# A four-layer graph network with a planned instruction order: q's factor moved into the copies, layer 2's statistics on ScalarE, six of eight divisions on ScalarE, other ranks

## Chip, cores and metric

The kernel runs on one core of a Trainium2 chip. The metric is the device time of one execution in microseconds; the time before is 3005.9 us, the median of three runs (3004.96 to 3010.77). The engines are named as in the profile: PE is TensorE (matmuls), PEld its weight loads, DVE is VectorE, ACT is ScalarE, POOL is GpSimd, and SP issues most DMAs.

## What is computed

The input x has 128 batches of 128 nodes with 512 features, all in 32-bit floats. Four layers follow, each with a residual sum and a layer norm; `adj` is one 128 x 128 matrix that all batches share.

```python
x = layernorm(x + (adj @ x) @ weight + bias)                 # layer 0
h = x @ W; e = leaky_relu(s1[:, None] + s2[None, :]) * adj   # layer 1: s1, s2 = h @ a1, h @ a2
x = layernorm(x + elu(softmax(e) @ h + beta * h))
x = layernorm(x + max over the last axis of relu(pre))       # layer 2, from adj and b
q, k, v = x @ w_qkv                                          # layer 3: 8 heads of 64
o = softmax(where(adj == 0, -inf, q @ k.T * 64**-0.5)) @ v
o = o @ w_proj + b_proj
x = layernorm(x + o + (o - mean(o)) * rstd(o) * gamma + beta)
```

In layer 2 the same matrix serves as W1 and W2, so its result for a node is one number: the greatest of its mixed features plus b, and at least 0. It is added to all 512 features of the node.

## The kernel before

A batch is a tile of 128 nodes by 512 features in one large SBUF tile, the arena, which is cut into units of 256 columns. Each of the 128 batches is a Python generator, `batch(i)`, that yields a request for an engine (`use("ACT", 0.48)`), with its cost in microseconds and the buffers it needs, and then issues instructions. The class `Plan` runs all generators at build time: it keeps a time for each engine and buffer, takes the request that can start first (ties go by urgency, then by rank, where a lower rank is served first), and so writes out the order in which each engine's instructions stand. The costs are multiplied by `SLACK` (1.1 for ACT, 1.05 for DVE), PE requests are planned `MARGIN` after their inputs are ready, and a request's rank is mostly the number of its batch, shifted by `SOFT`, `PROJ`, `SECTION` and, for the last groups, `SOON`. On the chip each engine works through its list in this fixed order and waits where an input is late.

The products with 512 x 512 weights are done for two batches at a time with seven block products instead of eight (`seven`, a Strassen-Winograd scheme). It needs sums of weight blocks, made once on POOL (`sums`, line 584), and differences of data blocks, made on POOL for each product (`differences`, line 901). The block products of layers 0, 1 and of the projection are issued at line 914, those of layer 3's q, k and v at line 963 (`section`, for a group of four batches). Their results come out of PSUM by an ACT copy (lines 818 and 881) and by a DVE addition onto what was copied before (805, 811, or 801 where a row sum is taken along). The chain is copy, next PE product, addition, so PE is tied to ACT and DVE within each product.

What a batch does, with its lines:

- Layer 0: mixing by `adj` on PE (386 with a transpose on DVE and a round trip through DRAM, or 367), products (914, or 359 for the first twelve batches), the bias on POOL (352), then `layernorm_sums`: ACT makes the squares with an accumulated sum (340), a small ACT instruction the variance (342), POOL its power of -0.5 (306), ACT the bias of the norm (345) and the norm (346). DVE only scales the row sum (335 or 337).
- Layer 1: logits on DVE (1142, 734 to 761) with exponentials on ACT (749) and two DMA round trips, mixing (367), products (914), ELU (1166, 1168, 1183), `layernorm_sums`.
- Layer 2: mixing (1193), the maximum on DVE (1196, 1199), its addition on ACT (1207), then `layernorm_dve`: DVE takes the statistics (293, 299, 301), POOL the power (306), DVE the norm (323).
- Layer 3: a transpose (1214) and a DMA round trip, q, k and v (963), scores (1040), the mask (1231), the maximum over each head's row (1239), eight exponentials on ACT with accumulated sums (1253), the reciprocal (1259), eight ACT instructions that multiply by it (1267), transposes (1271), a DMA round trip, the product with v (1061), a copy (1302), the projection (914; 359 and 1433 for the last four batches), and the two norms (1406, 1410, `layernorm_sums`, store at 1416).

The switches in question stand at the top of the file. `SCALED` is the number of heads whose division is done on ACT; the others are divided by one DVE instruction. `SUMS2` chooses for layer 2 between `layernorm_sums` (1) and `layernorm_dve` (0). `WHOLE` is the number of last batches whose softmax is done over all heads at once. `GUESTS` is the number of first batches whose input may lie in any free part of the arena. `RUN` holds batch i back until the group `RUN` before its own has its layer 3 inputs. `APART` is the number of last groups whose products with v are requested by themselves (`attend`), not in turns with the next group's scores (`tiled`).

The scale of the scores, 64 ** -0.5, is put into q's weights once, on POOL, before the weight sums of layer 3 are made:

```python
yield use("POOL", 5.8)
nc.gpsimd.tensor_scalar(
    wqkv_sb[:, :, :D], wqkv_sb[:, :, :D], HD**-0.5, None, op0=ALU.mult
)
```

Of the kernel before, what the change touches and what calls it, by code (L numbers as in the profile page):

```python
# [9 lines left out]
AF = mybir.ActivationFunctionType  # L10
ALU = mybir.AluOpType
# [5 lines left out]
D = 512  # L17
K = D // P
G = 4
APART = 6  # L20
FIRST = 0
PAIRS = 2
SOON = (0, 0, -2, 8, 12, 18)
WHOLE = 0
KEPT = 7
ATTENDS = 2
RUN = 8
SEVEN0 = 1
SUMS2 = 0
SCALED = 8  # L30
SEVEN1 = 1
SEVENP = 1
PLAIN = 4
GUESTS = 10
STICK = 0.4
CLOSE = 2900
SOFT = 10
PROJ = -6
SECTION = 12
PACE = 0  # L40
EAGER = 8
H = 8
HD = D // H
# [8 lines left out]
UNIT = 256  # L52
CAPS = {"x": 9, "xr": 2, "yT": 8, "v": 4, "qk": 10, "xT": 4}
SIZES = {"u": 1, "t": 2, "x": 2, "early": 2, "xr": 2, "yT": 2, "v": 4, "qk": 4, "xT": 4}
LAST, AHEAD = 16, 6
DIRECT = 12
LATER = 3
LANDED = 2.2
# [5 lines left out]
SP_ = 1.1  # L64
SLACK = {"PE": 1.0, "DVE": DVE_, "ACT": ACT_, "POOL": POOL_, "SP": SP_}
BORDERS = 0.1
MARGIN = 0.7
LAND, ROW_LAND = 2.8, 0.0053


# [158 lines left out]
def gnn_stack_kernel(  # L229
# [252 lines left out]
    def loads():  # L482
        yield use("SP", 0.4)
        adj_slot.append((yield use("SP", 0.0, "t")))
        adj_sb = buf(adj_slot[0], D)[:, :P]
        adj_slot.append(adj_sb)
        nc.sync.dma_start(adj_sb, adj)
        landing(adj_in, P // 4)
        yield from load(0, "ACT", nc.scalar)
        w0_slot.extend((yield use("SP", 0.0, lambda: ("qk", "qk"))))  # L490
        halves = [buf(slot, 2, D) for slot in w0_slot]
        w0_nat.extend(halves[k // 2][:, k % 2] for k in range(K))
        for k in range(K):
            yield use("SP", 0.43)
            nc.sync.dma_start(w0_nat[k], w0[k * P : (k + 1) * P])
            landing(w0_chunk[k], P)
        yield from load(1)
        yield use("SP", 0.43)
        nc.sync.dma_start(bias0_sb, rows(bias0, D))
        landing(bias0_in, P)  # L500
        for i in range(2, 4):
            yield from load(i)
        slot = yield use("SP", 1.1, "qk")
        matrix(w1_sb, w1)
        a_sb = buf(slot, 2, D)
        nc.sync.dma_start(a_sb, rows(a, 2 * D).rearrange("p (s f) -> p s f", s=2))
        landing(w1_in, (K + 2) * P)
        plan.start(logit_rows(a_sb, slot), 0)
        for i in range(4, 8):
            yield from load(i)  # L510
        yield use("SP", 5.6)
        permuted(w0_sb, w0)
        landing(w0_in, K * P)
        plan.start(layer0_sums(), 0)
        yield use("SP", 1.0)
        nc.sync.dma_start(beta1_sb, rows(beta1, 1))
        nc.sync.dma_start(
            b2_sb, bass.AP(tensor=b2.tensor, offset=b2.offset, ap=[[1, P], [1, 1]])
        )
        landing(scalars_in, 2 * P)  # L520
        for i in range(8, 14):
            yield from load(i)
        yield use("SP", 6.3)
        permuted(wqkv_sb, w_qkv)
        matrix(wproj_sb, w_proj)
        for dst, src in ((bproj_sb, b_proj), (gamma_sb, gamma), (beta3_sb, beta3)):
            nc.sync.dma_start(dst, rows(src, D))
        landing(w3_in, (4 * K + 3) * P)
        plan.start(weight_sums(), 0)
        for i in range(14, NB):  # L530
            yield from load(i)

# [53 lines left out]
    def weight_sums():  # L586

        yield w3_in
        yield use("POOL", 5.8)
        nc.gpsimd.tensor_scalar(  # L590
            wqkv_sb[:, :, :D], wqkv_sb[:, :, :D], HD**-0.5, None, op0=ALU.mult
        )
        for s in range(3):
            yield from sums(s)
        done(w3_ready)
        if SEVENP:
            yield from sums(4)
        done(wproj_ready)
# [192 lines left out]
        gr.xT[2] = buf(gr.slot["xT", 2], 1, 2, n)  # L791
        yield from differences(gr.block, gr.have, gr.used, 0.18 + 0.58 * gr.half, gr.first)

    def seven(rank, bx, wide, time, multiply, parts, finished, have, home, housed, slow=0.0, into=None):

        copy, sum_ = (0.45, 0.6) if wide == D else (0.24, 0.33)
        copy, sum_ = copy + slow, sum_ + slow

        def total(a, c, i, j):
            if into:  # L800
                nc.vector.scalar_tensor_tensor(  # L801
                    c, a, 1.0, c, op0=ALU.mult, op1=ALU.add, accum_out=into[j][i]
                )
            else:
                nc.vector.tensor_tensor(c, a, c, op=ALU.add)  # L805

        def kept(p, i, j, event):
            if into:
                yield use("DVE", sum_, urgent=True)
                for a, c in parts(p, i, j):  # L810
                    nc.vector.tensor_tensor(c, a, c, op=ALU.add)
                done(event)
                return
            got = yield use("ACT", copy, lambda: home(j), urgent=True)
            if got:
                housed(j, got)
            for a, c in parts(p, i, j):
                nc.scalar.copy(c, a)  # L818
            done(event)

        def keep(p, i, j):
            event = Event()
            plan.start(kept(p, i, j, event), rank)
            return event

        def added(p, kept, i, j, event):
            yield kept
            yield use("DVE", sum_, urgent=True)
            for a, c in parts(p, i, j):
                total(a, c, i, j)  # L830
            finished(j)
            done(event)

        def add(p, kept, i, j):
            event = Event()
            plan.start(added(p, kept, i, j, event), rank)
            return event

        def release(event, bank):
            yield event  # L840
            give(bank)

        x = bank(bx, D)[:, :wide]
        multiply(x, A11, B11, True)
        m1 = keep(x, 0, 0)

        bz = yield use("PE", time, "ps")
        z = bank(bz, D)[:, :wide]
        multiply(z, A12, B21, True, True)
        plan.start(release(add(z, m1, 0, 0), bz), rank)  # L850

        yield m1
        yield have[T2]
        yield use("PE", time)
        multiply(x, S2, T2)
        u2 = keep(x, 1, 0)

        yield have[T3]
        by = yield use("PE", time, "ps")
        y = bank(by, D)[:, :wide]  # L860
        multiply(y, S3, T3, True)
        yield u2
        yield have[T1]
        yield use("PE", time)
        multiply(x, S1, T1)
        u4 = keep(x, 1, 1)
        c22 = add(y, u4, 1, 1)
        yield u4
        yield use("PE", time)
        multiply(x, S4, B22, final=True)  # L870

        def last(bx):
            if into:
                yield use("DVE", sum_, urgent=True)
            else:
                yield use("ACT", copy, urgent=True)
            for a, c in parts(x, 0, 1):
                if into:
                    total(a, c, 0, 1)
                else:  # L880
                    nc.scalar.copy(c, a)
            give(bx)
            finished(1)

        plan.start(last(bx), rank)
        yield c22
        yield have[T4]
        yield use("PE", time)
        multiply(y, A22, T4, final=True)
        plan.start(release(add(y, u2, 1, 0), by), rank)  # L890
# [51 lines left out]
    def section(gr, s, before):  # L942
# [51 lines left out]
        def housed(j, got):  # L994
# [8 lines left out]
        done(gr.begun[s])  # L1003
        yield from seven(
            gr.first, bx, wide, time, multiply, parts, finished, gr.have, home, housed,
            0.0 if s == 2 or half == 1 else 0.07,
        )

    def tiled(gr, before, bs):
        yield gr.qk  # L1010
        waiting = list(range(before.size)) if before else []
        for b in waiting:
            yield before.rows[b]

        steps = [(score, bs[:2])]
        steps += [(attends, waiting[b : b + 2]) for b in range(0, len(waiting), 2)]
        steps += [(score, bs[b : b + 2]) for b in range(2, len(bs), 2)]
        was = None
        for do, batches in steps:
            n = len(batches)  # L1020
            slots = yield use(
                "PE", 0.87 * n, lambda: ("ps",) * (n if do is attends else 2 * n),
                late=0.0, urgent=True, follow=was is not None, kind=do.__name__,
            )
            was = do
            if do is attends:
                attends(before, batches, slots)
                continue
            for m, b in enumerate(batches):
                score(gr, b, slots[2 * m : 2 * m + 2])  # L1030
                done(gr.scored[b], 0.2 - 0.87 * (n - 1 - m))
# [58 lines left out]
    def batch(i):  # L1090
# [169 lines left out]
        if SCALED < H:  # L1260
# [2 lines left out]
                rs[:, SCALED:, None].to_broadcast([P, H - SCALED, P]), op=ALU.mult,  # L1263
            )
        for j in range(SCALED):
            yield use("ACT", 0.2)
            nc.scalar.activation(pr[:, j, :], pr[:, j, :], AF.Identity, scale=rs[:, j : j + 1])  # L1267
        halves = yield use("DVE", 1.22, lambda: ("t", "t"))
        turned = [buf(bt, Q, H // 2, S) for bt in halves]
# [250 lines left out]
```

## Time and profile before

| what | us |
|---|---|
| median of three runs | 3005.9 |
| the profiled execution | 3009.2 |
| its span, first to last instruction | 3007.5 |
| ACT, exponentials (line 1253), 1024 instructions | 404.8 |
| ACT, divisions (line 1267), 1024 instructions | 373.7 |
| DVE, statistics (line 293), 255 instructions | 173.8 |
| POOL, powers (line 306), 383 + 257 instructions | 247.1 + 166.3 |
| POOL, q's factor (line 590), one instruction | 5.5 |

The granted TensorE clock is 0.995 of full speed on average. HBM moves 142 GB/s, the DMA engines are busy about half of the time. A busy time is a sum over the records of a group; consecutive ACT instructions overlap by about 0.1 us in the records, so the time from one start to the next is a little shorter than the mean of one.

### The profile page before, as it was taken

What the parts mean: (1) busy time and instruction counts of PE and PEld (TensorE: products, weight loads), DVE (VectorE), ACT (ScalarE), POOL (GpSimd) and SP (SyncE); (2) the same over time, 40 slices, a digit from 0 to 9 for tenths busy, and PEclk for the clock granted to TensorE, in tenths of its full rate; (3) what the DMA queues carried; (4) which work ended last, traced back from release to release, by engine and by line L of the source; (5) the groups of instructions that cost most, each with busy time, mean ns of one, the idle gap of its engine ahead of it and who ended that gap; (6) DMA issues with size and microseconds to landing.
All of it is one profiled execution on the core that took longest, in us unless ns stands there. A gap on an engine that the chain in (4) does not pass through costs nothing. (4 is left out here: it accounts for less than half of the span.)

```text
span 3007.5 us, 54842 instructions
## 1 busy us (share of the span) xinstructions
PE 2950.5 (98%) x16503; PEld 2476.7 (82%) x16503; DVE 2554.8 (85%) x6023; ACT 2209.8 (73%) x6916; POOL 1886.0 (63%) x2050
## 2 busy tenths in 40 slices
PE   9899999999999999999999999999999999999997
PEld 5688788888888888888888888888888888888886
DVE  7998788888988888988898888988988988888676
ACT  4568677777677777777776777676886767777696
POOL 7855566566657666667565666656665655765545
PEclk9999999999999999999999999999999999999999
DMA  5445455355545555654555544646455644654353
GB/s 210 101 117 161 115 163 156 106 146 157 154 137 145 145 144 155 167 137 150 132 153 144 156 137 121 162 135 164 146 139 148 169 128 120 175 142 131 89 148 123
DMA packets 884104, 430.83 MB, mean 143 GB/s; under 512 B 572128, under 2 KB 785760, under 8 KB 883808
## 3 DMA queue, kind: packets, MB, share of 16 engines
q1 hardware_dynamic: 865376, 393.75, 48.6%
q10 hardware_dynamic: 18432, 33.56, 3.0%
q8 instruction: 133, 2.18, 0.3%
q14 instruction: 163, 1.34, 0.1%
HBM read 222.36 MB, written 204.80 MB: 142 GB/s over the span
## 5 line engine op out<-in xcount | busy, mean ns | idle before, releaser
L901 POOL TENSOR_TENSOR arena<-arena 128x256 f32<-128x256 f32 (+1 forms) x868 | 764.8, 890 | 300.3 <-PE ps L914 93.0
L914 PE MATMUL ps<-wsum_sb,arena 128*128 128x256 f32 x2208 | 553.5, 383 | 17.8 <-POOL arena L901 7.8
L914 PEld LDWEIGHTS ps<-wsum_sb,arena 128*128 128x128 f32 x2208 | 414.7, 191 | 105.9 <-issue 17.6
L914 PE MATMUL ps<-w_sb,arena 128*128 128x256 f32 x1952 | 489.7, 379 | 4.7 <-DVE arena L805 2.8
L306 POOL TENSOR_TENSOR sums<-sums,neghalf 128x1 f32<-128x1 f32 x383 | 247.1, 648 | 376.5 <-ACT sums L342 363.8
L963 PE MATMUL ps<-arena,wqkv_sb 128*128 128x256 f32 (+1 forms) x2112 | 481.4, 373 | 0.7 <-DVE arena L801 0.7
L805 DVE TENSOR_TENSOR arena<-ps,arena 128x256 f32<-128x256 f32 (+1 forms) x861 | 359.6, 442 | 140.7 <-ACT arena L818 67.9
L963 PEld LDWEIGHTS ps<-arena,wqkv_sb 128*128 128x128 f32 x2112 | 392.4, 190 | 64.1 <-issue 10.0
L818 ACT COPY arena<-ps 128x256 f32<-128x256 f32 (+1 forms) x861 | 311.6, 388 | 166.8 <-PE ps L963 95.7
L914 PEld LDWEIGHTS ps<-w_sb,arena 128*128 128x128 f32 x1952 | 369.4, 190 | 76.2 <-issue 17.5
L1253 ACT ACTIVATE arena<-arena,nmx 128x128 f32<-128x128 f32 x1024 | 404.8, 399 | 16.1 <-DVE nmx L1239 15.7
L1267 ACT ACTIVATE arena<-arena,rs 128x128 f32<-128x128 f32 x1024 | 373.7, 398 | 11.5 <-DVE rs L1259 7.1
L340 ACT ACTIVATE arena<-arena,sums 128x512 f32<-128x512 f32 x371 | 266.1, 717 | 156.4 <-DVE sums L335 96.2
L963 PE MATMUL ps<-arena,wsum_sb 128*128 128x256 f32 (+1 forms) x1584 | 359.4, 373 | 1.9 <-ACT arena L818 1.7
L963 PEld LDWEIGHTS ps<-arena,wsum_sb 128*128 128x128 f32 x1584 | 293.9, 190 | 50.6 <-issue 7.7
L346 ACT ACTIVATE arena<-arena,sums 128x512 f32<-128x512 f32 x383 | 311.6, 814 | 12.8
L306 POOL TENSOR_TENSOR n<-n,neghalf 128x1 f32<-128x1 f32 x257 | 166.3, 648 | 212.6 <-DVE n L301 205.6
L1142 DVE SCALAR_TENSOR_TENSOR arena<-arena,wa_rows 128x512 f32<-128x512 f32 x256 | 260.1, 1018 | 21.4 <-ACT arena L346 16.4
L352 POOL TENSOR_TENSOR arena<-arena,beta_sb 128x512 f32<-128x512 f32 x128 | 177.3, 1388 | 114.5 <-DVE arena L1214 103.5
L914 PE MATMUL ps<-wproj_sb,arena 128*128 128x256 f32 x992 | 244.7, 382 | 0.3 <-DVE arena L1231 0.3
L963 PE MATMUL ps<-wqkv_sb,arena 128*128 128x256 f32 x1024 | 243.4, 380 | 0.0
L963 PEld LDWEIGHTS ps<-wqkv_sb,arena 128*128 128x128 f32 x1024 | 194.5, 191 | 38.7 <-issue 10.1
(116 smaller groups left out, 5504.6 us busy)
## 6 DMA issues: line engine op xcount, KB each, us to landing
p_d<-arena SPq DMA_DIRECT2D x256, 256.0 KB
arena<-p_d SPq DMA_DIRECT2D x128, 512.0 KB
x_d<-arena SPq DMA_DIRECT2D x244, 256.0 KB
arena<-x_d SPq DMA_DIRECT2D x976, 64.0 KB
arena<-in_x SPq DMA_DIRECT2D x127, 256.0 KB
out<-arena ACTq DMA_DIRECT2D x127, 256.0 KB
x_s<-arena SPq DMA_DIRECT2D x121, 256.0 KB
arena<-x_s SPq DMA_DIRECT2D x121, 256.0 KB
```

Of the source, the lines that this page charges most:

```text
L306: nc.gpsimd.tensor_tensor(rstd, ve, neghalf, op=ALU.pow)
L340: nc.scalar.activation(buf_or_bank(unread), xb, AF.Square, bias=nm, accum_out=squares)
L346: nc.scalar.activation(xb, xb, AF.Identity, bias=nmr, scale=rstd)
L352: nc.gpsimd.tensor_tensor(dst, dst, other, op=ALU.add)
L805: nc.vector.tensor_tensor(c, a, c, op=ALU.add)
L818: nc.scalar.copy(c, a)
L901: nc.gpsimd.tensor_tensor(blocks(out), blocks(a), blocks(b), op=ALU.subtract)
L914: nc.tensor.matmul(p, t[:, k], w[:, k, :], start=first and k == 0, stop=final and k == 1, skip_group_check=True,)
L963: nc.tensor.matmul(to, lhs, rhs, start=first and j == 0 and k == 0, stop=final and k == 1, skip_group_check=True,)
L1142: nc.vector.scalar_tensor_tensor(unread, xb, 1.0, wa_rows[:, j, :], op0=ALU.mult, op1=ALU.mult, accum_out=gr.s[:, b, j : j + 1],)
L1253: nc.scalar.activation(pr[:, j, :], pr[:, j, :], AF.Exp, bias=nmx[:, j : j + 1], accum_out=sums[:, j : j + 1],)
L1267: nc.scalar.activation(pr[:, j, :], pr[:, j, :], AF.Identity, scale=rs[:, j : j + 1])
```

## The change

It does six things. The factor 64 ** -0.5 is no longer put into q's weights; instead `seven` gets an argument `scale`, and for q (s == 0 in `section`) its ACT copies become activations with that scale and its DVE additions multiply by it (`scalar_tensor_tensor`). The weight sums of layer 0 and layer 3 start with ranks 2 and 12 instead of 0. Layer 2 uses `layernorm_sums` with one accumulated row sum. Six of eight heads are divided on ACT, two by a DVE product, and the planner's cost of an ACT division goes from 0.2 to 0.29. The last four batches take the whole softmax: DVE adds the negated maximum to 1024 columns, ACT takes one exponential, DVE the sums. And the constants of the planner change. `ATTENDS_FIRST` is 0, so the order of steps in `tiled` stays.

```diff
-APART = 6
+APART = 7
-SOON = (0, 0, -2, 8, 12, 18)
-WHOLE = 0
+SOON = (-2, 0, -2, 6, 12, 18)
+WHOLE = 4
-RUN = 8
+RUN = 7
-SUMS2 = 0
-SCALED = 8
+SUMS2 = 1
+SUMS0 = 2
+SUMS3 = 12
+ATTENDS_FIRST = 0
+SCALED = 6
-GUESTS = 10
+GUESTS = 12
-SOFT = 10
-PROJ = -6
-SECTION = 12
+SOFT = 4
+PROJ = -5
+SECTION = 14
-LAST, AHEAD = 16, 6
+LAST, AHEAD = 20, 4
-MARGIN = 0.7
+MARGIN = 0.5
...
-        plan.start(layer0_sums(), 0)
+        plan.start(layer0_sums(), SUMS0)
...
-        plan.start(weight_sums(), 0)
+        plan.start(weight_sums(), SUMS3)
...
         yield w3_in
-        yield use("POOL", 5.8)
-        nc.gpsimd.tensor_scalar(
-            wqkv_sb[:, :, :D], wqkv_sb[:, :, :D], HD**-0.5, None, op0=ALU.mult
-        )
         for s in range(3):
             yield from sums(s)
...
+            elif scale:
+                nc.vector.scalar_tensor_tensor(c, a, scale, c, op0=ALU.mult, op1=ALU.add)
             else:
                 nc.vector.tensor_tensor(c, a, c, op=ALU.add)
+
+        def copied(c, a):
+            if scale:
+                nc.scalar.activation(c, a, AF.Identity, scale=scale)
+            else:
+                nc.scalar.copy(c, a)
...
             for a, c in parts(p, i, j):
-                nc.scalar.copy(c, a)
+                copied(c, a)
...
-            0.0 if s == 2 or half == 1 else 0.07,
+            0.0 if s == 2 or half == 1 else 0.07, scale=HD**-0.5 if s == 0 else None,
...
         for j in range(SCALED):
-            yield use("ACT", 0.2)
+            yield use("ACT", 0.29)
             nc.scalar.activation(pr[:, j, :], pr[:, j, :], AF.Identity, scale=rs[:, j : j + 1])
```

More of the change, by code (lines that the diff above doesn't have):

```diff
@@ L792, in gather, with seven @@
         yield from differences(gr.block, gr.have, gr.used, 0.18 + 0.58 * gr.half, gr.first)
-    def seven(rank, bx, wide, time, multiply, parts, finished, have, home, housed, slow=0.0, into=None):
+    def seven(rank, bx, wide, time, multiply, parts, finished, have, home, housed, slow=0.0, into=None, scale=None):
         copy, sum_ = (0.45, 0.6) if wide == D else (0.24, 0.33)
@@ L880, in last @@
                 else:
-                    nc.scalar.copy(c, a)
+                    copied(c, a)
             give(bx)
@@ L1015, in tiled @@
         steps = [(score, bs[:2])]
+        if ATTENDS_FIRST:
+            steps = []
         steps += [(attends, waiting[b : b + 2]) for b in range(0, len(waiting), 2)]
-        steps += [(score, bs[b : b + 2]) for b in range(2, len(bs), 2)]
+        steps += [(score, bs[b : b + 2]) for b in range(0 if ATTENDS_FIRST else 2, len(bs), 2)]
         was = None
```

## The prediction

> **What bounds the kernel now.** I read the engines' shares first, then the busy time by stage, then what TensorE (PE) waited for, then the costs of the instructions that the change moves, then the chain at the end.
>
> ```profile
> span 3007.5 us, 54842 instructions
> PE 2950.5 (98%) x16503; PEld 2476.7 (82%) x16503; DVE 2554.8 (85%) x6023; ACT 2209.8 (73%) x6916; POOL 1886.0 (63%) x2050
> ```
>
> PE is busy 98% of the span, and no PE instruction is added or removed: both programs list 8265. So the time can move only by PE's idle 57 us, by a slower clock, and by the tail. The next view says where the idle time lies (columns: stretch, its length, then busy time of PE, weight loads, DVE, ACT, POOL, then the clock).
>
> ```profile
> 0.00:60.00 60.00, 55.33 (x211) 31.92 (x211) 43.95 (x95) 26.00 (x63) 41.31 (x39) 1.00 0.66 244
> 60.00:160.00 100.00, 86.48 (x377) 65.65 (x378) 96.39 (x230) 59.66 (x150) 86.81 (x86) 0.95 0.39 95
> 200.00:1000.00 800.00, 790.26 (x4450) 666.52 (x4450) 672.43 (x1577) 590.09 (x1864) 483.37 (x524) 1.00 0.53 145
> 1000.00:2000.00 1000.00, 993.02 (x5525) 842.13 (x5522) 862.90 (x2049) 751.91 (x2365) 637.88 (x696) 1.00 0.53 145
> 2000.00:2700.00 700.00, 693.72 (x3935) 588.27 (x3934) 607.42 (x1433) 521.74 (x1651) 446.97 (x496) 1.00 0.55 149
> 2900.00:3008.00 108.00, 91.64 (x650) 76.62 (x649) 79.40 (x176) 84.34 (x294) 60.40 (x67) 0.94 0.45 137
> ```
>
> PE's idle time: 4.7 us to 60, 13.5 from 60 to 160, none to 200, 23.0 from 200 to 2700 (9.7, 7.0, 6.3), none to 2900, 16 after. From 60 to 160 DVE is busy 96% and POOL 87%, ACT only 60%: the ramp is where the two vector engines limit PE. In the middle none is full, and PE waits for single late hand-offs:
>
> ```profile
> PE ps L914 <- POOL arena L901: 6.3, 4, 4.4
> ...
> PE ps L914 <- ACT arena L818: 5.9, 6, 2.2
> PE ps L1193 <- ACT arena L346: 3.7, 4, 1.5
> PE ps L1193 <- DVE arena L801: 2.6, 2, 1.6
> PE ps L963 <- ACT arena L818: 2.0, 4, 1.0
> ```
>
> The first row is from the waits up to 200 us, the others from 200 to 2700 (total, times, longest). With the rows not shown, the middle holds 11.6 us behind ACT, 8.9 behind DVE, 1.5 behind POOL.
>
> **The change part by part.**
>
> ```profile
> L1267 ACT ACTIVATE arena<-arena,rs 128x128 f32<-128x128 f32 x1024 | 373.7, 398 | 11.5 <-DVE rs L1259 7.1 <-DVE logits L754 2.2 <-ACT arena L818 0.6
> L340 ACT ACTIVATE arena<-arena,sums 128x512 f32<-128x512 f32 x371 | 266.1, 717 | 156.4 <-DVE sums L335 96.2 <-DVE sums L337 46.2 <-PE ps L963 3.5
> L323 DVE TENSOR_SCALAR arena<-arena,n 128x512 f32<-128x512 f32 x128 | 87.4, 686 | 6.1 <-POOL n L306 5.6
> L740 DVE TENSOR_TENSOR arena<-arena,adj_cols 128x256 f32<-128x256 f32 x64 | 46.4, 725 | 2.2
> ```
>
> *Layer 2's statistics (SUMS2), load.* DVE loses per batch the statistics at L293 (0.68), L299 (0.18), L301 (0.15) and the scaling at L323 (0.69): 1.70 us, times 128 is 218. It gains L335 (0.14): 18. ACT gains the square pass with its accumulator read (0.82 from one start to the next at the end of the trace), L342 and L345 (0.30 each), L346 (0.81), and an accumulator read on the bias pass (0.2: 0.82 against L1168's 0.63, a pass of the same size without one): 2.43 us, times 128 is 311. POOL keeps its 128 powers (648 ns), which now wait for ACT's L342 instead of DVE's L301.
>
> *Division, six heads (SCALED).* ACT loses 256 instructions; six of them follow each other in 1.77 us in the chain, 0.295 each, so 76 us. DVE gains 128 products of 128x256 with both inputs in SBUF. The nearest row is L740: 0.42 at least, 0.73 on average, 1.43 at most, so 54, 93 or 183 us. I take 93.
>
> [...]
>
> *The last four softmaxes whole (WHOLE).* Per batch ACT exchanges eight exponentials (0.39 each) for one of 1024 columns (1.4, under two passes of L346), DVE gains an addition of 1024 columns (2.1, two L1410) and a reduction (1.2, L1239). Together ACT -7, DVE +13.
>
> *q's factor.* It removes one POOL instruction of 5.54 us at 47.1 us. 256 ACT copies become scaled activations: 0 to 45 ns more each (L1168's 627 against 582 for a copy of 512 columns), 0 to 12 us. 192 DVE additions become scalar_tensor_tensor from PSUM: L801 takes 412 ns, L805 413, so nothing.
>
> Sums: ACT 2210 + 311 - 76 - 7 + 12 = 2450 (81%); DVE 2555 - 218 + 18 + 93 + 13 = 2461 (82%); POOL 1880. No DMA is added: SP lists 2256 instructions in both programs. DVE and ACT become even, and both stay under PE. What this does to the time is asked by stage.
>
> *Ramp, up to 200 us.* The largest PE wait is 4.4 us at 95.9, for POOL's L901. POOL sits there behind a power whose input comes late from ACT, and ran sixteen weight sums (L584) of 1.3 to 1.7 us between 53 and 107. After it the clock is 0.67 from 100 to 110, and five 512-column matmuls cost 0.4 us more each, 2 us. Without the factor POOL is 5.5 us earlier, though it idled 4 us from 40 to 60. The lower rank lets L901 pass a sum, but the changed program still has the sums between the same L901s. I take 5 us; bounds 0 (the wait stays behind ACT) and 13.5 + 5 (all idle time and the slow clock). DVE's relief comes later: the first L293 ran near 109 us, and only 3.4 us of PE's loss come after that. I take 2. Ramp: -7.
>
> *Middle, 200 to 2700.* I scale the waits with each engine's idle share. ACT from 26.5% to 18.5%: 11.6 us times 1.43, +5.0. DVE from 15% to 18%: 8.9 times 0.83, -1.5. Against this, the order is planned with a cost per instruction, and the division's goes from 0.2 to 0.29 (times 1.1: 0.22 and 0.32), where the chain shows 0.295. So ACT ran 8 x 0.075 = 0.6 us per batch behind its plan, and now 6 x 0.024 = 0.15 ahead; lateness is what ends in ACT waits, and I take a third off their 16.6 us, -5.5. The other ranks, RUN, MARGIN (PE instructions are planned 0.5 us behind their inputs instead of 0.7) and the buffers of early loads only reorder; I take 0. They are bounded by all 22 us gone and by as much added. Middle: -2. Behind a late ACT instruction in its queue stand the copies L818 and L1302, and PE waits for both; DVE's L805 waits for L818 too.
>
> *End.*
>
> ```profile
> 2951.69 1.12 PE ps L1040 x16
> ...
> 2966.79 1.77 ACT arena L1267 x6
> ...
> 2983.48 0.29 ACT sums L342
> 2983.78 0.48 ACT arena L1302
> 2984.30 5.23 PE ps L359 x8
> ```
>
> After the last scores ACT is busy without a break from 2960 to 2970, the copy L1302 then stands behind an L342, PE waits 2.64 us, and its eight matmuls take 5.23 instead of 3.4 us at a clock of 0.83. WHOLE takes 8 x 0.39 + 8 x 0.295 = 5.5 us per batch on ACT down to 3.2, and adds 4.0 on DVE, which was idle 6.6 us of those ten. Best case -4.5 (wait and slow clock), worst +8 (DVE's two last batches in a row). I take -1.5.
>
> Together -7 - 2 - 1.5 = -10.5 us. The profiled execution has a span of 3007.5 and a time of 3009.2; so 2997.0 + 1.7 = 2998.7, and as it lies 3.3 above the median of the runs, 2995.4 there.
>
> **The rivals.** *Slower: ACT becomes late in the middle.* The longer layer-2 chain (three more ACT passes and a POOL power that POOL's queue waits for) holds the copies. Place: waits of L914 and L963 for L818 from 200 to 2700. Price: a wait of the longest kind (2.2 us) in every second of 33 groups is 36 us, less 10.5: about 3031. It decides from where ACT waits exceed 22 us, twice the present. For it: ACT rises most, and POOL already idles 364 us behind L342. Against it: from 2910 to 2940 ACT is busy 98 to 100%, and PE never waits. *No change:* the sums still hold the ramp, the waits wash out: 3003 to 3006. For it: the first L293 comes after the ramp's long waits. *A large gain:* ramp -13, middle -11, end -4.5: 2977. For it: DVE leads the ramp; against it: the middle's waits have many releasers.
>
> **How the numbers follow.** Forecast 0.42 (2988 to 3000), large gain 0.14, no change 0.16, slower 0.28. A measurement can tell about 0.2%, 6 us. Faster: 0.42 + 0.14; within: 0.16. The range 2977 to 3031 leaves out about 0.06 below and 0.12 above; the likeliest case's own is 2988 to 3000.
>
> **What would show it.** Right: DVE near 2460, ACT near 2450; PE's idle from 60 to 160 down from 13.5 to about 7, its middle idle near 21; no 4 us wait for L901. Wrong: the waits behind ACT over 22 us from 200 to 2700, new stretches of slow clock, or the last PE instruction more than 13 us ahead of the end.

## The result, and the profile after

The changed kernel takes 2995.4 us (median of 6 runs, 2993.9 to 2996.9), the kernel before 3005.4 in the same comparison: a ratio of 0.9964, 95% interval 0.9951 to 0.9977. That is 10 us less, or 0.36%.

The first view is the engines' shares of the profiled execution of the changed kernel, and then its stretches with the same columns as before (stretch, length, busy time of PE, weight loads, DVE, ACT, POOL, granted clock, DMA share, GB/s).

```profile
span 2993.1 us, 55166 instructions
PE 2941.6 (98%) x16503; PEld 2481.8 (83%) x16503; DVE 2457.0 (82%) x5775; ACT 2402.7 (80%) x7368; POOL 1873.3 (63%) x2049
```

```profile
0.00:60.00 60.00, 53.68 (x207) 31.45 (x207) 43.70 (x91) 25.55 (x63) 38.88 (x40) 1.00 0.71 251
60.00:160.00 100.00, 92.82 (x413) 72.66 (x414) 92.93 (x233) 74.55 (x195) 91.93 (x95) 0.97 0.45 110
200.00:1000.00 800.00, 789.63 (x4502) 671.62 (x4501) 649.26 (x1520) 652.51 (x2047) 476.16 (x526) 1.00 0.53 144
1000.00:2000.00 1000.00, 995.42 (x5592) 845.43 (x5591) 828.61 (x1971) 818.37 (x2520) 635.56 (x700) 1.00 0.54 147
2000.00:2700.00 700.00, 697.32 (x3861) 593.25 (x3860) 578.52 (x1376) 566.47 (x1742) 451.20 (x492) 1.00 0.53 144
2900.00:2994.00 94.00, 77.23 (x552) 63.28 (x550) 75.94 (x157) 58.31 (x157) 50.16 (x56) 0.93 0.44 135
```

The work has gone from DVE to ACT. In the ramp, 60 to 160 us, PE's idle time fell from 13.5 to 7.2 us, with DVE at 93 instead of 96% and ACT at 75 instead of 60%. From 200 to 2700 us it fell from 23.0 to 17.6; from 2700 to 2900 there are now 4.5 us where there were none.

PE's busy time fell too, by 9 us, though its instructions are the same: the same matmuls have longer records in some places, such as eight that take 5.4 us near the end at a granted clock of 0.72 and 3.6 us shortly before at full clock. So busy and idle time alone don't measure what PE loses, and I also worked out a loss that holds both. For each matmul it is the time to the next one's start, less the spacing that most matmuls of its size keep (216 ns for 256 columns, 429 for 512, 112 for 128, about 60 for scores and products with v). The spacings add up to 2905.2 us in every kernel here. What lies above is the loss. The table has it by stretch of the span (us), and in the last column the time from the last matmul's start to the end; the runs below the second row are those of the experiments:

```
             0-60  60-160  160-200  200-1000  1000-2000  2000-2700  2700-2900  2900-  tail
before        8.0    21.6      0.0      21.7       16.7       12.9        1.7    6.7  12.9
changed      10.4    10.7      0.0      19.6       13.1        8.1        6.6    7.4  12.1
r_factor      6.8    21.2      0.0      21.0       15.1       12.3        1.7    6.6  12.1
k_stats       9.4    21.2      0.9      26.7       19.8       15.3       11.5    9.3  12.1
k_div8        9.2    11.7      0.0      15.8        9.1        6.7        6.9    6.4  12.4
n_margin51    9.1    12.5      0.5      17.3       18.5        7.4        2.9   23.5   9.0
n_margin49    9.2    15.6      0.0      18.4       14.6       31.5       36.4   31.1   9.0
x_oa_wb      23.7    19.6      2.6      25.1       17.9        9.9       10.9    7.0  12.4
x_ob_wa       6.8    26.4      5.4      41.0       40.6       29.5       12.0   10.6  12.1
```

From before to changed the ramp gives 8.5 us, the middle 10.5, and from 2700 us on 4.8 are given back. What PE waited for from 200 to 2700 us in the changed kernel (total, times, longest):

```profile
PE ps L921 <- POOL arena L908: 5.5, 5, 3.0
PE ps L921 <- DVE arena L818: 3.3, 4, 1.1
PE ps L970 <- ACT arena L810: 1.9, 2, 1.8
PE ps L1202 <- DVE sums L338: 1.6, 1, 1.6
...
PE ps L921 <- ACT arena L812: 0.3, 1, 0.3
```

The line numbers have moved. Of the changed kernel, L921, L970, L1202 and L362 are the products 914, 963, 1193 and 359 of before, L908 is POOL's 901, L812 the ACT copy 818, L810 the same copy with q's scale, L806 and L818 the DVE additions 805 and 811, L338 the scaled row sum 335, L349 the norm 346 and L1311 the copy 1302. ACT, which does 193 us more, is waited for 2.2 us in all instead of 11.6; DVE 7.0 instead of 8.9; POOL 6.8 instead of 1.5. And the end, two instructions of ACT and then one row of PE in order of time (start, length, line, in brackets the idle time before it and what ended it):

```profile
2968.95 0.72 ACT L343 ACTIVATE arena<-arena,sums 128x512 f32<-128x512 f32 x1 [5.95 <-DVE sums L338]
...
2970.00 0.56 ACT L1311 COPY arena<-ps 128x512 f32<-128x512 f32 x1
```

```profile
2970.61 5.40 PE L362 MATMUL ps<-wproj_sb,arena 128*128 128x512 f32 x8 [2.84 <-ACT arena L1311]
```

The stall of before is still there: the copy L1311 stands behind a square pass that waits 5.95 us for DVE, PE waits 2.84 us, and the clock drops (0.72 from 2970 to 2976 us; the eight matmuls take 5.4 us, and 3.6 in the group before the waits).

### The profile page after: what moved, and what is told of

Same layout as the page of the kernel before. It is cut to its first block, busy times and chain, and to the rows that moved or that the text cites. A ratio compares the mean times of both kernels' runs of the same rounds, so it can differ in the third digit from the quotient of the medians.

```text
span 2993.1 us, 55166 instructions
## 1 busy us (share of the span) xinstructions
PE 2941.6 (98%) x16503; PEld 2481.8 (83%) x16503; DVE 2457.0 (82%) x5775; ACT 2402.7 (80%) x7368; POOL 1873.3 (63%) x2049
## 5 line engine op out<-in xcount | busy, mean ns | idle before, releaser
L908 POOL TENSOR_TENSOR arena<-arena 128x256 f32<-128x256 f32 (+1 forms) x868 | 763.0, 888 | 325.1 <-PE ps L921 82.3
L309 POOL TENSOR_TENSOR sums<-sums,neghalf 128x1 f32<-128x1 f32 x511 | 322.4, 633 | 511.5 <-ACT sums L345 504.5
L921 PE MATMUL ps<-wsum_sb,arena 128*128 128x256 f32 x2208 | 547.1, 381 | 13.5 <-POOL arena L908 8.0
L921 PEld LDWEIGHTS ps<-wsum_sb,arena 128*128 128x128 f32 x2208 | 415.6, 191 | 95.3 <-POOL arena L908 14.7
L921 PE MATMUL ps<-w_sb,arena 128*128 128x256 f32 x1952 | 482.2, 381 | 5.0 <-DVE arena L806 3.5
L970 PE MATMUL ps<-arena,wqkv_sb 128*128 128x256 f32 (+1 forms) x2112 | 480.8, 373 | 0.0
L812 ACT COPY arena<-ps 128x256 f32<-128x256 f32 (+1 forms) x892 | 338.3, 395 | 158.7 <-PE ps L921 91.0
L970 PEld LDWEIGHTS ps<-arena,wqkv_sb 128*128 128x128 f32 x2112 | 393.5, 191 | 67.3 <-issue 16.2
L343 ACT ACTIVATE arena<-arena,sums 128x512 f32<-128x512 f32 x499 | 357.0, 716 | 114.5 <-DVE sums L338 94.1
L921 PEld LDWEIGHTS ps<-w_sb,arena 128*128 128x128 f32 x1952 | 371.0, 191 | 79.9 <-issue 20.2
L349 ACT ACTIVATE arena<-arena,sums 128x512 f32<-128x512 f32 x511 | 415.9, 814 | 17.1
L806 DVE TENSOR_TENSOR arena<-ps,arena 128x256 f32<-128x256 f32 (+1 forms) x669 | 291.7, 452 | 133.5 <-ACT arena L812 57.0
L1262 ACT ACTIVATE arena<-arena,nmx 128x128 f32<-128x128 f32 x992 | 388.3, 394 | 10.2 <-DVE nmx L1248 10.2
L970 PE MATMUL ps<-arena,wsum_sb 128*128 128x256 f32 (+1 forms) x1584 | 356.6, 374 | 5.6 <-POOL arena L908 3.7
L970 PEld LDWEIGHTS ps<-arena,wsum_sb 128*128 128x128 f32 x1584 | 293.8, 191 | 57.6 <-issue 11.0
L1276 ACT ACTIVATE arena<-arena,rs 128x128 f32<-128x128 f32 x768 | 281.1, 395 | 12.4 <-DVE rs L1268 8.2
L355 POOL TENSOR_TENSOR arena<-arena,beta_sb 128x512 f32<-128x512 f32 x128 | 170.3, 1334 | 141.3 <-DVE arena L1223 130.1
L1151 DVE SCALAR_TENSOR_TENSOR arena<-arena,wa_rows 128x512 f32<-128x512 f32 x256 | 224.7, 879 | 21.7 <-ACT arena L349 17.0
L970 PE MATMUL ps<-wqkv_sb,arena 128*128 128x256 f32 x1024 | 242.0, 380 | 0.0
L921 PE MATMUL ps<-wproj_sb,arena 128*128 128x256 f32 x992 | 240.5, 384 | 0.2
L970 PEld LDWEIGHTS ps<-wqkv_sb,arena 128*128 128x128 f32 x1024 | 194.4, 190 | 31.5 <-issue 4.7
L355 POOL TENSOR_TENSOR arena<-arena,bproj_sb 128x512 f32<-128x512 f32 x124 | 173.8, 1411 | 65.1 <-ACT arena L812 54.2
```

The lines of the kernel that those rows point to most:

```text
L309: nc.gpsimd.tensor_tensor(rstd, ve, neghalf, op=ALU.pow)
L343: nc.scalar.activation(buf_or_bank(unread), xb, AF.Square, bias=nm, accum_out=squares)
L349: nc.scalar.activation(xb, xb, AF.Identity, bias=nmr, scale=rstd)
L355: nc.gpsimd.tensor_tensor(dst, dst, other, op=ALU.add)
L908: nc.gpsimd.tensor_tensor(blocks(out), blocks(a), blocks(b), op=ALU.subtract)
L921: nc.tensor.matmul(p, t[:, k], w[:, k, :], start=first and k == 0, stop=final and k == 1, skip_group_check=True,)
```

## The experiments

Two kinds. In the first, a part is undone, or one constant moved, and the plan is drawn again; in the second, the matmuls keep their places and only the work changes. Each result is the median, then its ratio to the kernel before in the same comparison, with the 95% interval.

**Parts undone, the plan drawn again.**

```diff
 u_factor:  + use("POOL", 5.8) and the factor on wqkv_sb;  - scale=HD**-0.5
 u_stats:   -SUMS2 = 1   +SUMS2 = 0
 u_div8:    -SCALED = 6  +SCALED = 8
 u_ranks:   the constants APART, SOON, RUN, GUESTS, SOFT, PROJ, SECTION, LAST, AHEAD, MARGIN of before
```

> The changed kernel with q's factor put back into the weights (one POOL instruction of 5.5 us, plain copies for q); everything else as changed. Theory of the prediction (the ramp gains because POOL is relieved): PE's loss from 60 to 160 us rises by about 5 us, the time is about 3000 us. Rival A (layer 2's statistics and the middle carry the gain): no change against the changed kernel, 2995 within 3 us. Rival B (each edit only draws another order, with no worth of its own): anywhere within 6 us of 2995, and the difference does not sit in the ramp.

3053.6 us, ratio 1.0157 (1.0142 to 1.0172). This kernel's output is wrong. One block of the projection's weights, which holds a sum, is loaded anew for the last four batches as soon as one pair of batches is done with it (at 2948.6 us), and in this order another pair comes after that: it is projected with the new block. The amount of work is the same, so the time still tells of the order. No theory allowed 58 us for a POOL instruction of 5.5, and the ramp, 60 to 160 us, holds 3.5 of them. The largest single wait is 18.1 us, for the DMA that brings the softmax of a last batch.

> The changed kernel with layer 2's statistics back on DVE; everything else as changed. DVE gains about 200 us of work (to about 2657, 89%), ACT loses about 300 (to about 2090, 70%). Theory of the prediction (DVE's relief is worth 2 us in the ramp and a part of the middle's waits): about 3002 us. Rival A (the relief of DVE carries the gain): 3006 us or more, with PE waiting for DVE in the ramp and the middle. Rival B (a new order, no worth of its own): 2995 within 6 us.

3005.5 us, 0.9996 (0.9987 to 1.0005): 10 us slower than the changed kernel, where the prediction's theory gave about 7 and rival A 11 or more. By the profiles the ramp loses 8 us more than in the changed kernel, the middle 2.6, and the stretch from 2900 us on 6.5; 4.5 come back from 2700 to 2900.

> The changed kernel with all eight heads divided on ACT again, at the planner's cost of 0.29; everything else as changed. ACT gains about 80 us (to about 2480, 83%), DVE loses 93 (to about 2365, 79%). Theory of the prediction: ACT's waits rise by its smaller idle share, 2 to 4 us in the middle, about 2998 us. Rival A (DVE's relief carries the gain): faster than the changed kernel, 2990. Rival B: 2995 within 6 us.

3074.4 us, 1.0226 (1.0211 to 1.0242): 79 us for 256 small ACT instructions. From 200 to 2700 us PE waited 25.9 us in ten waits for the layer norm ahead of layer 2 (L1202 for L349).

> The changed kernel with the planner's constants of before (APART, SOON, RUN, GUESTS, SOFT, PROJ, SECTION, LAST, AHEAD, MARGIN); SUMS2, SCALED, WHOLE, the factor in the copies, the ranks of the weight sums and the cost 0.29 as changed. Theory of the prediction (these constants only reorder, worth nothing): 2995 within 3 us. Rival C (the constants carry the gain, the moved work does not): 3003 us or more, lost mostly between 200 and 2700 us. Rival B: within 6 us of 2995.

3010.4 us, 1.0019 (1.0009 to 1.0029). The work is the changed kernel's. By the profiles 14 us are lost from 2900 us on, and none in the middle.

Rival B as it stood here, within 6 us of 2995, failed in all four, and most of these losses do not sit where the undone work is. So the next question was what a new order costs when nothing else changes.

**The same work in an order drawn again.**

```diff
-MARGIN = 0.5
+MARGIN = 0.51   (n_margin51)
+MARGIN = 0.49   (n_margin49)
```

> The changed kernel with MARGIN 0.51 instead of 0.5: every instruction is the same work, but the plan is drawn anew (5742 of 8263 PE instructions stand elsewhere). Theory of the prediction (an order as such is worth little): 2995 within 4 us. Rival B (each newly drawn order has a price of its own, and the edits undone one by one before paid that): 3005 us or more, with the loss in other stages than the ramp.

3007.5 us, 1.0000 (0.9990 to 1.0010).

> The same with MARGIN 0.49. Theory of the prediction: 2995 within 4 us. Rival B: 3005 us or more, and not the same as with 0.51.

3075.9 us, 1.0229 (1.0213 to 1.0244). Where its time goes, from the waits of PE from 2700 us on:

```profile
PE ps L1202 <- ACT arena L349: 25.4, 4, 15.1
PE ps L362 <- ACT arena L1311: 6.1, 1, 6.1
PE ps L1442 <- ACT arena L1311: 6.1, 1, 6.1
```

PE stands up to 15.1 us before a layer 2 product whose batch is late, with other batches' products behind it in its list. From 2000 to 2700 us it loses another 23 us more than the changed kernel. A hundredth of a microsecond in one constant costs 12 or 80 us, so rival B holds in the form that it has for these two runs: a drawn order has a price of its own, larger than the whole change. The total times of the four runs above therefore don't price the parts that were undone.

**Order and work crossed.** Two kernels issue other instructions under the same planned requests, so all 8263 matmuls stay in place.

```diff
 x_oa_wb (order of changed, work of before; also plain copies for q and eight divisions):
+        nc.gpsimd.tensor_scalar(wqkv_sb[:, :, :D], ..., HD**-0.5, ...)   # no request of its own
 ...
         yield use("DVE", 0.07, follow=True)
+        nc.vector.bn_stats(...); mean_var(...)
 ...
         yield use("ACT", 1.03)
+        nc.vector.tensor_scalar(xb, xb, mv[:, 0:1], rstd, op0=ALU.subtract, op1=ALU.mult)
 x_ob_wa (order of before, work of changed; also scaled copies for q and six divisions):
         yield use("DVE", 1.0)
+        nc.vector.tensor_scalar(nm, total, ...); nc.scalar.activation(squared, xb, AF.Square, ...)
 ...
         yield use("DVE", 0.59)
+        nc.scalar.activation(nmr, ...); nc.scalar.activation(xb, xb, AF.Identity, bias=nmr, scale=rstd)
```

> The order of the changed kernel (all 8263 matmuls in the same places), with the work of the kernel before: the factor on POOL and plain copies, layer 2's statistics and norm on DVE, eight divisions on ACT. WHOLE stays 4. Theory of the prediction (the moved work carries the gain): 3003 to 3008 us. Rival B (the order carries it): 2993 to 2999. Rival D (an order fits only the work that it was planned for): over 3010, with PE waiting for DVE in layer 2.

3032.2 us, 1.0079 (1.0063 to 1.0096). One flaw: the factor came to stand too early in POOL's list, where it waits 16 us for its weights to arrive, and that alone holds PE 16.7 us in the first 60 us. The loss there is 13 us over the changed kernel's; without it some 3019 remain, an estimate. From 200 to 2700 us PE waits 11.7 us for DVE, against 7.0 in the changed kernel; little of it is in front of layer 2's products.

> The order of the kernel before (all 8263 matmuls in the same places), with the work of the changed kernel: the factor in q's copies, layer 2's statistics and norm on ACT (the squares, which nobody reads, are written as 16-bit numbers into a tile of their own), six divisions on ACT and two on DVE. WHOLE stays 0, and fewer buffers for small results. Theory of the prediction (the moved work carries the gain): 2993 to 2999 us. Rival B (the order carries it): 3003 to 3008. Rival D (an order fits only its own work): over 3010, with PE waiting for ACT.

3090.2 us, 1.0274 (1.0258 to 1.0289). PE's waits from 200 to 2700 us:

```profile
PE ps L923 <- ACT arena L814: 21.4, 16, 3.5
PE ps L972 <- ACT arena L812: 10.3, 9, 2.1
PE ps L1204 <- ACT arena L349: 9.3, 10, 2.1
```

Rival D holds: both crossings are slower than both kernels. ACT is busy 2399 us here and 2403 in the changed kernel, and yet PE waits over 40 us for it instead of 2: the ACT passes of layer 2 stand in places that were planned for DVE, ahead of copies that PE needs. This kernel also has fewer buffers for small results; what that adds was not measured by itself.

**Single parts, the order kept.**

```diff
 r_factor (order and work of before, but):
         yield use("POOL", 5.8)
-        nc.gpsimd.tensor_scalar(wqkv_sb[:, :, :D], ...)        # and scale in q's copies
 k_stats (order and work of changed, but): layer 2 on DVE, as in x_oa_wb
 k_div8  (order and work of changed, but):
-        nc.vector.tensor_tensor(pr[:, SCALED:], ..., rs[:, SCALED:, None]..., op=ALU.mult)
         for j in range(SCALED):
             yield use("ACT", 0.29)
+            for m in (j,) if j < SCALED - 1 else range(j, H):
+                nc.scalar.activation(pr[:, m, :], pr[:, m, :], AF.Identity, scale=rs[:, m : m + 1])
```

> The kernel before, every engine's order kept, with q's factor alone moved: the POOL instruction of 5.5 us is left out of its place, q's copies and additions carry the scale. Theory of the prediction (POOL's 5.5 us are worth 5 us in the ramp): 3000 us against 3005. Rival A (POOL waits for ACT there anyway, and idled just before): 3004 to 3006. A loss can only come from q's copies, at most 12 us of ACT time in all: up to 3008.

3003.3 us, 0.9992 (0.9983 to 1.0001). The loss up to 160 us is 1.6 us smaller. PE's longest wait of the ramp did not move:

```profile
PE ps L922 <- POOL arena L909: 5.9, 4, 4.4
```

The interval runs from a gain of 5 us to none, with 2 to 3 the likeliest, so the total doesn't decide between the prediction's 5 us and rival A's 1 us at most. The wait does: the 5 us were to come from it, and it is as long without the factor.

> The changed kernel, all matmuls in the same places, with layer 2's statistics and norm alone put back on DVE (the square pass of ACT is left out, its slot stays empty; DVE's instructions stand where the plan has the DVE scaling and the last ACT pass). Theory of the prediction: 2 us in the ramp and some in the middle, 2998 to 3003. Rival D (an order fits only its own work): over 3008, with PE's new waits behind DVE.

3030.2 us, 1.0079 (1.0065 to 1.0092), 35 us over the changed kernel, as rival D said. Its ramp, 60 to 160 us, looks like that of before again: PE is busy 86.39 us (86.48 before, 92.82 changed) and DVE 96.22 (96.39, 92.93). But the halves of the ramp differ. These are before, changed and k_stats:

```profile
60.00:110.00 50.00, 39.69 (x152) 27.30 (x152) 48.80 (x101) 27.91 (x71) 45.68 (x40) 0.90 0.41 96
110.00:160.00 50.00, 46.79 (x226) 38.35 (x226) 47.58 (x130) 31.75 (x79) 41.14 (x47) 1.00 0.36 94
```

```profile
60.00:110.00 50.00, 43.04 (x175) 31.45 (x176) 49.06 (x108) 28.25 (x75) 44.64 (x42) 0.93 0.41 100
110.00:160.00 50.00, 49.78 (x240) 41.20 (x239) 43.87 (x126) 46.30 (x121) 47.30 (x54) 1.00 0.49 120
```

```profile
60.00:110.00 50.00, 42.23 (x180) 30.51 (x180) 49.02 (x103) 26.24 (x68) 44.59 (x42) 0.97 0.41 100
110.00:160.00 50.00, 44.16 (x199) 35.55 (x198) 47.20 (x128) 27.52 (x65) 39.19 (x46) 0.93 0.48 117
```

Up to 110 us k_stats keeps most of the gain, and DVE is as full in all three (48.8 to 49.1 of 50 us); after 110 it loses more than before did. The loss in all runs that bear on this (us):

```
                                       60-110  110-160  200-2700
before                                   16.5      5.2      51.3
r_factor   order of before               16.1      5.1      48.4
x_ob_wa    order of before, all work     16.1     10.2     111.1
changed                                   9.6      1.0      40.8
k_stats    its order, layer 2 on DVE     10.6     10.5      61.8
x_oa_wb    its order, work of before     11.3      8.3      52.9
u_stats    drawn again, layer 2 on DVE    9.5      9.0      43.4
u_factor   drawn again, factor on POOL    8.1      6.1      63.9
u_ranks    drawn again, old constants    12.0      2.3      40.0
u_div8     drawn again, eight on ACT     11.9      0.8      93.4
n_margin51 drawn again                   10.9      1.6      43.2
n_margin49 drawn again                   10.9      4.7      64.5
```

So the ramp's gain has two parts. Up to 110 us it comes with every new order, whether layer 2 is on DVE, the factor on POOL or the constants are the old ones, and it is absent from the order of before even with all the work moved. What these new orders share, and the order of before lacks, are the ranks of the weight sums (and the cost of 0.29, and WHOLE, which concerns the end); the ranks are the likely cause, but they were not tried by themselves. From 110 us on, about where layer 2's statistics begin (at 110.0 us in the kernel before), the gain is lost whenever they are put back on DVE (8.3 to 10.5), also in an order drawn for that (u_stats). With them on ACT in an order drawn for it, the loss is 0.8 to 4.7, but 6.1 in u_factor. In the middle, u_stats keeps three quarters of the gain with layer 2 on DVE, so that gain is not shown to be layer 2's. Beyond the ramp, the loss of k_stats from 200 to 2700 is 21 us over the changed kernel's, in an order that was planned for other work; drawn anew with the same work (u_stats) the whole kernel is 25 us faster than this.

> The changed kernel, all matmuls in the same places, with the division of the last two heads alone put back on ACT, behind the six others (ACT gains 76 us that the plan does not know of, DVE loses 93). Theory of the prediction (each hand-off has some slack, ACT's waits grow by a third): 2998 to 3002. Rival A (DVE's relief decides): 2990 to 2995. Rival D: over 3008, with PE waiting for ACT's copies as with the other work in the order of before.

2986.2 us (2985.3 to 2986.6), 0.9931 (0.9917 to 0.9944). It is faster than both kernels: the division of the last two heads on DVE, a part of the change, costs 9 us in its order. The loss from 200 to 2700 falls from 40.8 to 31.6 and is level elsewhere. PE's waits there for DVE's additions L818, 3.3 us in the changed kernel, are

```profile
PE ps L921 <- DVE arena L818: 0.4, 1, 0.4
```

and ACT, with 61 us more and unplanned, is waited for 1.9 us. The same work in an order drawn anew was u_div8 with 3074 us: 88 us apart by the order alone.

**One stall of the end.**

```diff
-        b_t1 = yield use("DVE", 2.0, "t")
+        b_t1 = yield use("DVE", 2.0 if i < NB - 8 else 3.0, "t")
```

> The changed kernel with one cost of the plan raised, for the last eight batches alone: 3.0 instead of 2.0 for the two DVE passes of the norm (L1415, L1419). No matmul moves; on ACT the copy L1311 now stands ahead of the square pass that waits for DVE. If PE's wait of 2.8 us at 2970 us and the slow clock after it (5.4 instead of 3.6 us for eight matmuls) are on the path that ends last: 3 to 4 us less, 2991 to 2992. Rival (DVE's passes for the last batches end as late as before): 2994 to 2996.

3000.3 us, 0.9979 (0.9970 to 0.9988): 5 us slower, against both expectations. The copy moved ahead, and the 2.84 us are gone, but the next copy fell behind and the last product waits for it:

```profile
PE ps L1442 <- ACT arena L1311: 3.9, 1, 3.9
```

The tail from the last matmul's start grew from 12.1 to 14.5 us. The stall went to a later place on the same chain. The profiles put 3.5 us of the loss there; the rest lies scattered.

## Why the prediction came out, point by point

*The bound.* Right: PE's instructions and spacing are the same 2905.2 us in every kernel, and all differences are waits and slow clock above it.

*The loads.* DVE was put at 2461 us, and is 2457.0; the nearest row for the two-head product, L740's mean of 0.73 us, fits (0.72, from 0.42 to 1.54). ACT was put at 2450, and is 2402.7: by its records it gained 319 us in layer 2 and lost 93 by the division, where I had 311 and 76, and consecutive records overlap by about 0.1 us, which a sum of busy time leaves out. One of the passes that left DVE, L323, was as uneven as the product that came: 0.50 to 1.55 us, 0.69 on average.

*Ramp, -7.* Measured 8.5 us of loss, the sum nearly right and its make-up partly wrong. PE's idle time from 60 to 160 came to 7.2 us, where "about 7" was the sign, and the 4 us wait for L901 is gone (POOL is waited for 0.9 us there), as the prediction said. But "I take 5 us" for q's factor failed: by itself the factor left that wait at 4.4 us, and with the factor back on POOL (u_factor) the loss up to 110 us is as small as in the changed kernel. What the prediction set aside there, "the lower rank lets L901 pass a sum, but the changed program still has the sums between", or something else in the new orders, is worth the 7 us up to 110. For DVE's relief "I take 2" was too small and its place right: it comes after 110 us and is 4 us between the two kernels. Two readings on the way were off: from 99.7 to 106.6 us, around the end of the long wait, the granted clock was 0.51, which by estimate loses over 3 us and not 2; and the eight matmuls of the end take 3.6 us in the same records, not 3.4.

*Middle, -2.* Measured 10.5 us of loss, 5.4 of it idle time. The scaling of waits with an engine's idle share failed: ACT's waits were to stay near 11 and fell to 2.2, POOL's rose from 1.5 to 6.8. And "ACT loses 256 instructions" was counted as a help; k_div8 shows that this part costs 9 us in this order. What the 10.5 us come from is open: the term's own parts failed, and runs drawn again lie on both sides. Whether the cost of 0.29 made the plan truer, as I argued, was not tried by itself, since any change of it draws the order anew.

*The constants: "only reorder; I take 0".* This is the step that failed most. With them as before the same work takes 3010.4 us, 15 more, and with MARGIN moved by 0.01 it takes 3007.5 or 3075.9. What a mere reordering is worth is not near 0 but from 12 to 80 us in these runs, and its bounds in the prediction, 22 us either way, were too narrow.

*End, -1.5.* Measured 4.8 the other way from 2700 us on (4.9 and 0.7 more loss, 0.8 less tail). The stall at the copy that was to go is still there; what WHOLE does by itself was not tried.

So the total was met by terms that made up for each other: against its own term the middle came out 8.5 us better, the ramp 1.5 better and the end 6.3 worse, -14.2 us together between the two profiled spans where -10.5 was forecast. Between the medians it is 10.1, since the profiled execution of before lies 3.8 us above its median and that of the changed kernel on it. That the median fell on the forecast to a tenth is luck. Of the gain, about 4 us of the ramp go with layer 2's move from DVE to ACT, as k_stats and u_stats show; the rest is not shown to be any part's work, and up to 110 us it comes with the order. No run shows which constant of the plan brings it. The rival that ACT becomes late did not come true in the order planned for it, and did in the order that was not (x_ob_wa).

What stays open: what makes a drawn order good. Six plans with the same work or one part undone lie between 3005 and 3076 us, none below the changed kernel. The kernel before was not drawn again with a constant that means nothing, so how good its order is among its like isn't known, and the 10 us may be the difference of two orders more than of two amounts of work. Single ranks, the ranks of the weight sums and RUN were not tried alone.

## What to carry to other kernels

Where a planner writes the order, a part's worth can't be read from undoing it and planning again: first draw the plan anew with a change that means nothing, and see how far the time moves. To price a part within an order, keep the order and change only what is issued; and compare the loss in halves of a stage before giving a gain to a part, since equal totals can hide different places. In these runs the moved work cost over 80 us when it was put into places planned for the old work (x_ob_wa against before), and in its own order it was 10 us faster than before. A product moved to DVE (82% busy) for balance cost 9 us more than the same work on an ACT that was busier still (83%).

## What was not expected of the hardware

In the order of the changed kernel, ACT at 83% busy (2464 of 2983 us, k_div8) delayed PE less than ACT at 73% in the kernel before: 1.9 us of waits from 200 to 2700 against 11.6. An engine's share of busy time said little about who waits for it; the places of its instructions did.
